# Folding query weights with a head in each half of TensorE's columns, and three moved steps, in a two-layer gated cross-attention block

## The chip, the cores and the metric

The kernel runs on one NeuronCore of one Trainium2 chip. The metric is the device time of one execution in microseconds. Three runs of the kernel before took 1539.04, 1533.52 and 1535.97 us: the median is 1535.97 us. The engines are named as in the profile: PE is TensorE (PEld its weight loads), DVE is VectorE, ACT is ScalarE, POOL is GpSimd, and SP is SyncE, which here only issues DMAs.

## The reference, cut to what matters

The model has two layers, each a gated cross-attention and a gated feed-forward part. All data are float32; x is 16 blocks of 128 tokens by 512. The change touches layer 0's attention and the first steps of layer 0's feed-forward part:

```python
# layer 0 attention: H = 16 heads, K = D_C = 128, D_CQ = 384, R = 64
q_hk  = (hidden_q @ Wq.T).reshape(b, s, H, K)
q_big = einsum('bshk,hkq->bshq', q_hk, w_kc_q)
kv_rope = kv_c * cos + rotate_half(kv_c) * sin
q_r = einsum('bshq,hqr->bhsr', q_big, W_qr)
k_r = einsum('bld,hdr->bhlr', kv_rope, W_kr)
attn = softmax(einsum('bhsr,bhlr->bhsl', q_r, k_r))
ctx_lat = einsum('bhsd,hkd->bshk', einsum('bhsl,bld->bhsd', attn, kv_rope), w_kc_kv)
out = ctx_lat.reshape(b, s, H * K) @ Wo.T

# layer 0 feed-forward: 8 experts of rank 16, two chosen per token
base_h1 = x @ W1 + b1
t1 = einsum('td,erd->ter', x, A1);  l1 = einsum('ter,efr->tef', t1, B1) * 2
a = gelu(base_h1[:, None] + l1);    mix = (a * combine).sum(1)
```

The three matrices between x and q_r (Wq, w_kc_q, W_qr) do not depend on the tokens, so they can be multiplied together once: for each head, M = w_kc_q @ W_qr is 128 x 64, and Wq_head.T @ M is 512 x 64.

## The kernel before, in words

**The query fold (lines 470 to 575).** The 16 heads are taken as 8 pairs. `load_middle(p)` (L471) loads a pair's w_kc_q, turned so that its 384 inner rows lie on partitions in three chunks (`wcq`, 384 KB a pair), and its W_qr (`wqr`, 192 KB). `load_inner(p)` (L484) loads its 256 rows of Wq (`wq`, 512 KB). All go through SP's queue, which issues in order; each tile has three buffers, so a pair's loads wait until the pair three places ahead has been used. `fold_first(p)` (L505) makes M: for each head j of the pair, three matmuls over the chunks with `wcq` of that head stationary (128 columns) and both heads' `wqr` moving (2 x 64 columns); one of the two 64-column results is the head's own, and DVE copies it to `m_sb`. `fold_second(p)` (L520) makes Wq_head.T @ M in four matmuls a head, which ACT copies to the folded weights `fq`. The first fold of pair p+1 stands ahead of the second fold of pair p (L550), so that DVE's copy has time.

In the same loop, group 0's keys and queries are made: `key` (L406, one matmul of 512 columns a pair) and `query` (L409, four a pair). Keys need the rotated latents: `load_kv(0)` (L379, called at L495, after the loads of the first pair and of the second pair's middle weights) loads them through SP, `rope` (L385) rotates them in five operations on POOL, and TensorE turns them (`kvtr`, L556). Queries need the normalised tokens: `layernorm_T` (L140) has DVE take the statistics of four blocks, normalise them (`xn`, two buffers), TensorE turn them (`xtr`), and ACT and DVE copy them out by turns (`evacuate`, L81).

**Product tiles.** PSUM is held in three pools of 512-column tiles: `mm` (four), `tr` (two) and `acc` (two). A step that takes a tile waits until the step that had it two or four places earlier has been read out.

**Layer 0's attention (lines 825 to 980)** has an order written out by hand: from L827 on TensorE, DVE's main steps and SP keep program order. `fold_outward(p)` (L592) multiplies w_kc_kv and Wo for heads p and p+8 into a near (`tr`) and a far (`acc`) tile; DVE copies part of the near product and makes two differences (L600, L605, L606), ACT copies the far product (L601), and the last difference reads both. `score(b)` makes a block's scores in four tiles; `soften(b, t)` is four exponentials on ACT with a product on POOL; `block` turns 32 x 32 blocks on DVE; `carry` moves them by DMA. `turn(v)` (L447) turns two normalised blocks through two `tr` tiles, the first copied out by ACT and the second by DVE. At L838 `turn(2)` stands ahead of `fold_next(7)`, the last outward fold.

**The step to the feed-forward part.** In the last round of the attention loop (`u == last`) the last products of the attention are made by `project(v, n)` (L718). `spread(first)` (L357, called at L952 between projects 1 and 5) makes t1 for the first group of tokens: four matmuls of 512 columns into a `tr` tile, then two scalings on DVE, one for each chosen expert, which read the tokens' choice `selT`. Behind the loop the layer's next loads are issued (x, `b2_sb`, and others), DVE makes a difference `b2_d` of the loaded `b2_sb` (L1000, the profile's `b_d`), and then `up_pair` (L1032) makes two feature chunks of base_h1 by seven products of half size each (`hs` and `ht` tiles, sums on DVE at L1053 to L1063), and `adapt_pair` (L1073) makes four `l` products from t1, adds base (L1088) and takes the gelu. `up_pair` and `adapt_pair` alternate over eight pairs of chunks.

Of the kernel before, what the change touches and what calls it, by code (L numbers as in the profile page):

```python
# [9 lines left out]
F32 = mybir.dt.float32  # L10
# [5 lines left out]
P = 128  # L16
# [7 lines left out]
NPAIR = H // 2  # L24
R = 64
QC = 3
# [16 lines left out]
def kernel(  # L43
# [9 lines left out]
    nc = tc.nc  # L53
# [9 lines left out]
    def mm_tile(name):  # L63
        return ps_mm.tile([P, 512], F32, tag="mm", name=name)

    def tr_tile(name):
        return ps_tr.tile([P, 512], F32, tag="tr", name=name)
# [13 lines left out]
    def evacuate(dst, src):  # L81

        flip[0] ^= 1
        if flip[0]:
            pin(nc.vector.tensor_copy(dst, src))  # L85
        else:
            nc.scalar.copy(dst, src)  # L87


    ident = const.tile([P, P], F32, name="ident")  # L90
# [283 lines left out]
    with tc.tile_pool(name="a0", bufs=2) as ap, tc.tile_pool(name="a0s", bufs=3) as sp:  # L374
# [4 lines left out]
        def load_kv(g):  # L379
            kv = ap.tile([P, GB, P], F32, tag="kv", name=f"kv_{g}", bufs=1)  # L380
            b = place(g * GB)
            send(kv, kvc[b : b + GB].rearrange("b l d -> l b d"))
            return kv
# [84 lines left out]
        with tc.tile_pool(name="fold", bufs=3, side="right") as fp:  # L468
            loaded = {}

            def load_middle(p):  # L471

                wcq_p = fp.tile([P, 2, QC, P], F32, tag="wcq", name=f"wcq_{p}")
                wqr_p = fp.tile([P, 2, QC, R], F32, tag="wqr", name=f"wqr_{p}")
                hs = slice(2 * p, 2 * p + 2)
                wcq_in = wcqT[hs].rearrange("h (p c) k -> p h c k", c=QC)
                wqr_in = wqr[hs].rearrange("h (p c) r -> p h c r", c=QC)

                for j in ((0, 1) if p == 0 else (slice(0, 2),)):
                    nc.sync.dma_start(out=wcq_p[:, j], in_=wcq_in[:, j])  # L480
                    nc.sync.dma_start(out=wqr_p[:, j], in_=wqr_in[:, j])
                loaded[p] = wcq_p, wqr_p

            def load_inner(p):  # L484
                wq_p = fp.tile([P, 2, D], F32, tag="wq", name=f"wq_{p}")
                nc.sync.dma_start(
                    out=wq_p,
                    in_=wq[2 * p * P : (2 * p + 2) * P, :].rearrange("(h p) d -> p h d", p=P),
                )
                loaded[p] = wq_p, *loaded[p]  # L490

            load_middle(0)
            load_inner(0)
            load_middle(1)
            kv_0 = load_kv(0)  # L495
            nc.scalar.dma_start(out=cos_sb, in_=cos_t)
            nc.scalar.dma_start(out=sin_sb, in_=sin_t)
            for n in range(GB):
                nc.scalar.dma_start(out=xs[n], in_=x[place(n)])
            nc.scalar.dma_start(out=wkr_sb, in_=wkr)  # L500
            nc.scalar.dma_start(out=gates[:, 0:2], in_=g_x.partition_broadcast(P))
            nc.scalar.dma_start(out=gates[:, 2:4], in_=g_f.partition_broadcast(P))
            nc.scalar.activation(gates, gates, AF.Tanh)

            def fold_first(p):  # L505


                _, wcq_p, wqr_p = loaded[p]
                m_sb = fp.tile([P, 2, R], F32, tag="m", name=f"m_{p}")
                for j in range(2):  # L510
                    m_ps = mm_tile(f"m_ps{p}_{j}")
                    for c in range(QC):
                        nc.tensor.matmul(
                            m_ps[:, : 2 * R], wcq_p[:, j, c, :], wqr_p[:, :, c, :],
                            start=(c == 0), stop=(c == QC - 1),
                        )
                    nc.vector.tensor_copy(m_sb[:, j, :], m_ps[:, ts(j, R)])
                return m_sb

            def fold_second(p, m_sb):  # L520
                wq_p = loaded[p][0]
                for j in range(2):
                    f_ps = mm_tile(f"f_ps{p}_{j}")
                    for c in range(ND):
                        nc.tensor.matmul(
                            f_ps[:, ts(c, P)], wq_p[:, j, ts(c, P)], m_sb,
                            start=True, stop=True,
                        )
                    nc.scalar.copy(
                        fq[:, :, ts(2 * p + j, R)],  # L530
                        f_ps.rearrange("p (c r) -> p c r", r=P)[:, :, ts(j, R)],
                    )

            load_middle(2)
            for p in range(1, 3):
                load_inner(p)
            m_next = fold_first(0)
            kvr_0 = rope(0, kv_0)
            for p in range(NPAIR):
                m_now = m_next  # L540
                if p + 3 < NPAIR:
                    load_middle(p + 3)
                    load_inner(p + 3)
                if p + 4 == NPAIR:
                    for n in range(GB, KEPT):
                        nc.sync.dma_start(out=xs[n], in_=x[place(n)])
                if p == 0:
                    fold_second(p, m_now)
                if p + 1 < NPAIR:
                    m_next = fold_first(p + 1)  # L550
                if p:
                    fold_second(p, m_now)
                else:
                    tr = tr_tile("kvtr_0")
                    for i in range(GB):
                        nc.tensor.transpose(tr[:, ts(i, P)], kvr_0[:, i, :], ident)  # L556
                    kvT_0 = ap.tile([P, GT], F32, tag="kvT", name="kvT_0", bufs=1)
                    evacuate(kvT_0, tr)
                k_ps = tr_tile(f"k_ps0_{p}")
                key(k_ps, p, kvT_0)  # L560
                for v in range(2):
                    evacuate(k_r[v][p], k_ps[:, ts(v, 2 * P)])
                if p == 0:
                    xnT_0 = layernorm_T("a0", 0)
                q_ps = tr_tile(f"q_ps0_{p}")
                query(q_ps, p, xnT_0)
                for v in range(2):
                    evacuate(q_r[v][p], q_ps[:, ts(v, 2 * P)])
                if p == NPAIR - 2:
                    deviations(2)  # L570
                    normalise(2)
                    roped_1 = rope(1, load_kv(1))
# [252 lines left out]
        def fold_next(p):  # L825
            fold_outward(p, outward[p])
            if p + 5 < NPAIR:  # L827
                outward.append(load_outward(p + 5))

        score(0)  # L830
        for p in range(7):
            fold_next(p)
            if p % 2 == 0:
                soften(0, p // 2)
                if p:
                    block(0, p // 2 - 1)
        score(1)
        turn(2)  # L838
        fold_next(7)
        block(0, 3)  # L840
        carry(0)
        soften(1, 0)
# [23 lines left out]
        last = NB // 2  # L866
        for u in range(1, last + 1):
# [80 lines left out]
            if u != last - 1:  # L948
                project(v, 1)
            soft_step(now, 3)  # L950
            if u == last:
                spread(first)  # L952
            project(v, 5)
            soft_step(now, 4)
            if u < last:
# [19 lines left out]
            if u == last - 2:  # L975
                first = measure(0)
# [481 lines left out]
    q = first  # L1458
    for g in range(NG):
        last = g == NG - 1  # L1460
        held = None
        for m in range(NF // 2):
            bases = up_pair(q, m)
            if held is not None:
                adapt(q, m - 1, held)
            held = adapt_pair(q, m, bases)
            if g > 0 and m == 3:
                for b in range((g - 1) * GB, g * GB):
                    moments1(b)
        if last:  # L1470
            deviations1(slice(0, g * GB))
            aqo_sb = wp.tile([P, 2 * ND, D], F32, tag="w16", name="aqo_sb")
            for n, w in enumerate((a_wqT, a_woT)):
                send(aqo_sb[:, n * ND : (n + 1) * ND, :], w.rearrange("(c p) d -> p c d", p=P))
            xb = fh.tile([P, H, P], F32, tag="T", name="xb_a1_0")
            standard(xb, 0, mv1, rstd1, "a1", q.mixed)
            tokens(0, xb)
        else:
            nxt = measure(g + 1)
            blocks(nxt, fh.tile([P, ND, GB, P], F32, tag="T", name=f"xb_f0_{g + 1}"),  # L1480
                   q.mixed)
            turn_blocks(nxt)
        down(q, 0)
        adapt(q, NF // 2 - 1, held)
        bias_out(q)
        second_ranks(q)
        if last:
            break
        for n in range(1, 7):
            down(q, n, {  # L1490
                2: lambda: route_parts(nxt), 6: lambda: spread(nxt),
            }.get(n))
            if n == 2:
                route(nxt)
                quarter_tokens(nxt)
            elif n == 3:
                send_chosen(nxt)
        q = nxt
# [169 lines left out]
```

## Time and profile before

| what | value |
|---|---|
| median of three runs | 1535.97 us (1533.52 to 1539.04) |
| the profiled execution's own time | 1537.8 us |
| its span, first to last instruction | 1536.0 us |
| mean granted TensorE clock | 0.996 |
| TensorE's first fold, L513 | 96 passes, 14.8 us busy |
| TensorE's second fold, L525 | 128 passes, 17.8 us busy |
| DMA moved | 161.39 MB |

The profile is of one execution; its times are counted from the start of its span. A float32 matmul shows as two passes, so 6 matmuls are x12; a transpose on TensorE shows as one. Passes overlap, and the end of each is modelled: the pace of a run of matmuls is read from the start of one group to the start of the next, not from the busy time. In the timeline a line has the start, the time to the group's end, the engine and line, what is written and read, the count, and in brackets the time that the engine stood idle before and what ended it. In the waits a line has who waited for whom, the total in microseconds, the number of waits and the longest. In the windows a line has the stretch, its length, the busy time of PE, PEld, DVE, ACT and POOL with their counts, the granted clock of TensorE, the share of the DMA engines and GB/s.

### The profile page before, as it was taken

The page shows a single profiled execution, that of the slowest core. Times are in us where ns is not written, and L with a number is a line of the kernel's source. Part 1 is how long each engine was busy: PE and PEld are TensorE (multiplying, and loading weights), DVE is VectorE, ACT ScalarE, POOL GpSimd, SP SyncE. Part 2 cuts the span into 40 slices and gives each one's busy share as a digit, 9 for nine tenths or more (in the row PEclk, how much of TensorE's full clock was granted, in tenths as well). Part 3 has the DMA queues.
Part 4 walks back from the last instruction along what each step waited for, and adds up shares of the span by engine and source line. Part 5 has one row for each costly group of instructions (what it writes and reads, how often), then busy time and mean ns, then how long its engine had stood idle before and what let it go on. Part 6 is the DMA issues. An engine that isn't in the chain of part 4 may idle for free.

```text
span 1536.0 us, 19400 instructions
## 1 busy us (share of the span) xinstructions
PE 1490.6 (97%) x6768; PEld 1005.2 (65%) x6768; DVE 837.6 (55%) x1727; ACT 433.2 (28%) x1425; POOL 435.9 (28%) x437
## 2 busy tenths in 40 slices
PE   7999999999999999999999999999999799999998
PEld 5667778878877666876687667866765344444444
DVE  2264554554565556565565557455657675666422
ACT  2262433443240222022201221122034553545210
POOL 2052533632531233114321332043222221222100
PEclk9999999999999999999999999999999999999999
DMA  8435567444546621732255114521544442233402
GB/s 280 124 86 91 143 177 176 97 113 93 99 67 159 236 72 56 164 118 72 72 141 147 69 70 118 155 73 48 157 91 110 76 67 58 31 69 56 90 14 69
DMA packets 372017, 161.39 MB, mean 105 GB/s; under 512 B 299344, under 2 KB 347216, under 8 KB 369744
## 3 DMA queue, kind: packets, MB, share of 16 engines
q1 hardware_dynamic: 370624, 158.44, 41.1%
q10 hardware_dynamic: 1296, 1.71, 0.3%
q8 instruction: 54, 0.88, 0.2%
q14 instruction: 43, 0.35, 0.1%
HBM read 106.35 MB, written 18.09 MB: 81 GB/s over the span
## 4 chain that ended last, share of the span: by engine, by line
PE 88%; DVE 5%; SPq 2%; DMA 2%; ACT 1%; issue 1%; POOL 0%; DVEq 0%; POOLq 0%; ACTq 0%
PE y_ps L165 15%; PE fy_ps L165 12%; PE q_ps L165 10%; PE t_ps L165 8%; PE l_ps L165 7%; PE hs_ps L165 7%; PE ht_ps L165 5%; PE c_ps L165 4%; PE vx_ps L165 3%; PE h_ps L165 3%; PE my_ps L165 3%; PE s_ps L165 3%; PE k_ps L165 2%; SPq L175 2%; PE o_ps L165 2%
## 5 line engine op out<-in xcount | busy, mean ns | idle before, releaser
L1092 POOL TENSOR_TENSOR near<-base,a 128x512 f32<-128x512 f32 x32 | 42.6, 1330 | 346.2 <-ACT base L1089 207.1
L197 POOL TENSOR_TENSOR e<-e,rden_a 128x512 f32<-128x512 f32 x64 | 66.5, 1039 | 245.4 <-DVE rden_a L195 242.7
L165 PE MATMUL l_ps<-t,b_sb 128*128 128x512 f32 x256 | 116.8, 599 | 3.3 <-DVE base L1053 3.3
L671 POOL TENSOR_TENSOR e<-e,rden_a 128x512 f32<-128x512 f32 x64 | 66.1, 1039 | 184.6 <-DVE rden_a L669 184.6
L165 PE MATMUL q_ps<-xnT_a,fq 128*128 128x256 f32 (+1 forms) x448 | 115.9, 410 | 0.0
L664 ACT ACTIVATE e<-s_ps,nmx_a 128x128 f32<-128x128 f32 x256 | 90.3, 385 | 81.7 <-DVE nmx_a L653 39.3
L1089 ACT ACTIVATE a<-a 128x512 f32<-128x512 f32 x64 | 40.3, 630 | 257.1 <-DVE a L1088 257.1
L190 ACT ACTIVATE e<-e,nmx_a 128x128 f32<-128x128 f32 x256 | 98.8, 387 | 32.6 <-DVE nmx_a L185 32.5
L1088 DVE TENSOR_TENSOR a<-l_ps,base 128x512 f32<-128x512 f32 x64 | 44.0, 687 | 106.4 <-PE l_ps L165 106.4
L165 PEld LDWEIGHTS q_ps<-xnT_a,fq 128*128 128x128 f32 x448 | 84.8, 190 | 24.5 <-issue 11.5
L165 PEld LDWEIGHTS l_ps<-t,b_sb 128*128 128x128 f32 x256 | 49.1, 192 | 63.7 <-issue 56.9
L1154 DVE SCALAR_TENSOR_TENSOR x<-fy_ps,gw,x 128x256 f32<-128x256 f32 x112 | 46.4, 475 | 76.4 <-PE fy_ps L165 76.4
L165 PE MATMUL fy_ps<-ring,far 128*128 128x256 f32 x384 | 87.2, 380 | 0.0
L165 PE MATMUL y_ps<-fo_raw,c 128*128 128x256 f32 x384 | 85.8, 380 | 0.9 <-DVE c L85 0.9
L738 DVE SCALAR_TENSOR_TENSOR x<-y_ps,gates,x 128x256 f32<-128x256 f32 x112 | 48.6, 476 | 64.1 <-PE y_ps L165 64.0
L165 PEld LDWEIGHTS fy_ps<-ring,far 128*128 128x128 f32 x384 | 72.6, 190 | 13.6 <-issue 3.9
L165 PEld LDWEIGHTS y_ps<-fo_raw,c 128*128 128x128 f32 x384 | 72.3, 190 | 11.1 <-ACT c L87 1.0
L165 PE MATMUL ht_ps<-T,ring 128*128 128x256 f32 x256 | 65.7, 379 | 0.0
L165 PE MATMUL t_ps<-base,a_sb 128*128 128x512 f32 x128 | 65.4, 592 | 0.0
L165 PE MATMUL t_ps<-a,a_sb 128*128 128x512 f32 x128 | 65.4, 592 | 0.0
L165 PE MATMUL q_ps<-xnT_a,aqo_sb 128*128 128x512 f32 x128 | 59.7, 617 | 4.8 <-DMA xnT_a<-late 4.8
L165 PE MATMUL y_ps<-fo_sums,c 128*128 128x256 f32 x256 | 60.8, 386 | 1.4 <-DVE c L85 0.8
(241 smaller groups left out, 2926.2 us busy)
## 6 DMA issues: line engine op xcount, KB each, us to landing
ring<-w SPq DMA_DIRECT2D x32, 896.0 KB, 4.5
eT<-eb SPq DMA_DIRECT2D x336, 64.0 KB, 2.3
ring<-w SPq DMA_DIRECT2D x16, 1024.0 KB, 5.7
ring<-in_f_w SPq DMA_DIRECT2D x12, 1024.0 KB, 5.4
late<-eb SPq DMA_DIRECT2D x80, 64.0 KB, 2.3
wq<-in_wq SPq DMA_DIRECT2D x8, 512.0 KB, 5.3
quarters<-in_f_w SPq DMA_DIRECT2D x32, 128.0 KB, 2.7
w<-sums SPq DMA_DIRECT2D x8, 512.0 KB, 3.4
```

The lines of the kernel that those rows point to most:

```text
L165: ins = nc.tensor.matmul(*args, **kw)
L175: ins = nc.sync.dma_start(out=dst, in_=src)
L190: nc.scalar.activation(dst[:, ts(i, P)], src[:, ts(i, P)], AF.Exp, bias=nmx[:, i : i + 1], accum_out=den[:, i : i + 1],)
L197: nc.gpsimd.tensor_tensor(d3, d3, rden.unsqueeze(2).to_broadcast([P, 4, P]), ALU.mult)
L664: nc.scalar.activation(e[:, ts(i, P)], s_ps[:, ts(i, P)], AF.Exp, bias=nmx[:, i : i + 1], accum_out=den[:, i : i + 1],)
L671: nc.gpsimd.tensor_tensor(e3, e3, rden.unsqueeze(2).to_broadcast([P, 4, P]), ALU.mult)
L738: pin(nc.vector.scalar_tensor_tensor(dst, y_ps, gate_x[0], dst, ALU.mult, ALU.add))
L1088: nc.vector.tensor_tensor(a, l_ps, base, ALU.add)
L1089: nc.scalar.activation(a, a, AF.Gelu_apprx_tanh)
L1092: nc.gpsimd.tensor_tensor(mix, base, second, ALU.add)
L1154: nc.vector.scalar_tensor_tensor(dst, y_ps[:, ts(i, half)], q.first[:, t : t + 1], dst, ALU.mult, ALU.add,)
```

## The change

Four edits. First, `fold_first` makes M transposed: `wqr` of a head is stationary (64 columns), `wcq` moves (128 columns), and head j writes partitions 64 j to 64 j + 63 of one 128 x 128 product, so that the two heads of a pair use the two halves of TensorE's columns; the chunks are the outer loop and the heads the inner. DVE copies the product (`m_T`), and a new step, `fold_turn`, transposes it on TensorE and copies it on DVE to the same `m_sb` as before. `fold_turn` stands at once behind the first fold for pair 0, and behind the second fold of the pair before for all others. Second, group 0's latents are loaded ahead of pair 0's Wq and pair 1's weights. Third, the last outward fold stands ahead of `turn(2)`. Fourth, the first group's `spread` stands behind the first `up_pair` instead of between projects 1 and 5.

```diff
@@ load order
             load_middle(0)
+            kv_0 = load_kv(0)
             load_inner(0)
             load_middle(1)
-            kv_0 = load_kv(0)
@@ fold_first
-                m_sb = fp.tile([P, 2, R], F32, tag="m", name=f"m_{p}")
-                for j in range(2):
-                    m_ps = mm_tile(f"m_ps{p}_{j}")
-                    for c in range(QC):
+                m_ps = mm_tile(f"m_ps{p}")[:, :P]
+                for c in range(QC):
+                    for j in range(2):
                         nc.tensor.matmul(
-                            m_ps[:, : 2 * R], wcq_p[:, j, c, :], wqr_p[:, :, c, :],
+                            m_ps[ts(j, R)], wqr_p[:, j, c, :], wcq_p[:, j, c, :],
                             start=(c == 0), stop=(c == QC - 1),
                         )
-                    nc.vector.tensor_copy(m_sb[:, j, :], m_ps[:, ts(j, R)])
+                m_T = fp.tile([P, P], F32, tag="mT", name=f"mT_{p}", bufs=1)
+                nc.vector.tensor_copy(m_T, m_ps)
+                return m_T
+
+            def fold_turn(p, m_T):
+                tr = mm_tile(f"mtr_{p}")[:, :P]
+                nc.tensor.transpose(tr, m_T, ident)
+                m_sb = fp.tile([P, 2, R], F32, tag="m", name=f"m_{p}", bufs=2)
+                nc.vector.tensor_copy(m_sb.rearrange("p j r -> p (j r)"), tr)
                 return m_sb
@@ the loop over pairs
-            m_next = fold_first(0)
+            m_next = fold_turn(0, fold_first(0))
...
                 if p + 1 < NPAIR:
-                    m_next = fold_first(p + 1)
+                    m_T = fold_first(p + 1)
                 if p:
                     fold_second(p, m_now)
...
+                if p + 1 < NPAIR:
+                    m_next = fold_turn(p + 1, m_T)
                 k_ps = tr_tile(f"k_ps0_{p}")
@@ layer 0's attention
         score(1)
+        fold_next(7)
         turn(2)
-        fold_next(7)
@@ the attention loop
             soft_step(now, 3)
-            if u == last:
-                spread(first)
             project(v, 5)
@@ layer 0's feed-forward loop
             bases = up_pair(q, m)
+            if g == 0 and m == 0:
+                spread(q)
```

Up to the scheduled part (the fold) a planner orders the instructions of each engine by the dependences; by the order that it emits, the last of pair 3's six first-fold matmuls stands behind the first query of group 0, and pair 6's middle weights are issued on SP ahead of the last of four token loads.

## The prediction

> **What bounds the kernel now.** I read the page first: its engine line and the chain of work that ended last.
>
> ```profile
> PE 1490.6 (97%) x6768; PEld 1005.2 (65%) x6768; DVE 837.6 (55%) x1727; ACT 433.2 (28%) x1425; POOL 435.9 (28%) x437
> PE 88%; DVE 5%; SPq 2%; DMA 2%; ACT 1%; issue 1%; POOL 0%; DVEq 0%; POOLq 0%; ACTq 0%
> ```
>
> TensorE is the bound: what shortens its stream, or fills one of its gaps, shortens the kernel, and what other engines gain or lose counts only through a gap. Then the waits of TensorE, for the four places that the diff touches.
>
> ```profile
> PE l_ps L165 <- DVE base L1053: 3.3, 1, 3.3
> PE kvtr L556 <- POOL kvr L400: 2.1, 1, 2.1
> PE o_ps L165 <- ACT xnT_a L87: 1.8, 1, 1.8
> PE f_ps L525 <- DVE m L517: 1.2, 1, 1.2
> ```
>
> Each of the three reorderings aims at one of the first three. Last, the granted clock, in windows: one gap pulls it to half, another does not.
>
> ```profile
> 18.00:19.00 1.00, 0.36 (x2) 0.36 (x3) 0.00 (x0) 0.00 (x0) 0.59 (x1) 0.79 1.07 371
> 21.00:22.00 1.00, 1.00 (x4) 0.59 (x3) 0.22 (x1) 0.00 (x0) 0.00 (x0) 0.50 1.05 360
> 512.00:513.00 1.00, 1.00 (x2) 0.34 (x1) 0.97 (x2) 0.99 (x2) 0.00 (x0) 0.50 1.19 386
> 97.00:99.00 2.00, 1.89 (x5) 0.88 (x6) 0.70 (x3) 1.12 (x7) 0.15 (x1) 1.00 0.00 0
> ```
>
> The column before the DMA share is the clock. It is 0.50 from 18.6 to 22.0 us, after the 2.06 us wait for kvr, and from 510.1 to 513.5 after the 3.27 us wait for base: 3.4 us each, 1.7 us lost. After the 1.82 us gap at 95 to 97 it stays at 1.00.
>
> **Part 1: the first fold in steady state.** One pair in the timeline of TensorE:
>
> ```profile
> 64.42 1.50 PE L513 MATMUL m_ps<-wqr,wcq 128*128 128x128 f32 x12
> 65.75 1.95 PE L525 MATMUL f_ps<-m,wq 128*128 128x128 f32 x16
> 67.54 1.02 PE L165 MATMUL k_ps<-kvT,wkr_sb 128*128 128x512 f32 x2
> 68.40 3.60 PE L165 MATMUL q_ps<-xnT_a,fq 128*128 128x512 f32 x8
> ```
>
> From start to start m takes 1.33 us (6 matmuls of two passes, 0.22 each), f 1.79, k 0.86, q 3.44. Afterwards the same 6 matmuls have 64 stationary columns each, two heads in the two halves. No row has 64 columns; the nearest is layer 1's values, four column groups of 32 at the same 128 rows and 128 moving columns:
>
> ```profile
> 1231.75 1.08 PE L165 MATMUL o_ps<-eT,v 128*32 128x128 f32 x32
> 1232.76 0.70 PE L165 MATMUL q_ps<-xnT_a,aqo_sb 128*128 128x512 f32 x1
> ```
>
> 16 matmuls in 1.01 us: four rounds at 0.22 are 0.88, so all four groups run at once, and 0.13 is lost on entering and leaving. For two halves: 3 rounds, 0.66 + 0.13 = 0.79 us. Bounds: 0.66 (free entry) and 1.33 + 0.13 = 1.46 (halves take turns). I take 0.79, nearest to that row: 0.54 saved. The transpose costs 0.12: eight xtr transposes go from 23.60 to 24.58. Net 0.42 us a pair.
>
> The Trainium skill, "TensorEngine Tiling (Array Packing)", section "Tiling Modes", says that a change of tiling mode drains TensorE. This case's trace agrees as far as the 0.13 us above; it gives no price, so the sum stays.
>
> DVE's two 128x64 copies (0.22 us each) become two of 128x128, between 0.22 and 0.42 (the 128x256 rows): 0.3. The one ahead of the transpose lies under f (1.79 us), the one behind it under k and q (4.3 us), and DVE is busy 1.2 to 2.0 of each 10 us from 40 to 70. If that cover were gone, a pair would pay 0.6. PSUM tiles stay at four a pair. Weight loads are still issued two pairs ahead, and DMA idles from 60 to 70. Pairs 4 to 7: 4 x 0.42 = **1.7 us**; pair 3, whose steady part before is still 5 of 6 matmuls and after only one, **0.6 us**.
>
> **Part 2: kv first, and the start.** kv's issue at 7.24 us lands 7.2 us later, at 14.4; rope takes 4 us on POOL (14.59 to 18.58), and TensorE stands.
>
> ```profile
> 18.64 1.12 PE L556 MATMUL kvtr<-ident,kvr 128*128 128x128 f32 x4 [2.06 <-POOL kvr L400]
> 19.55 1.91 PE L513 MATMUL m_ps<-wqr,wcq 128*128 128x128 f32 x8
> 27.06 3.67 PE L165 MATMUL q_ps<-xnT_a,fq 128*128 128x512 f32 x8
> ```
>
> Moved ahead of wq_0 and pair 1's loads on SP's in-order queue, kv lands about 8.9 (wq_0's 512 KB took 3.26 us, from 7.23 to 10.49; kv has half), kvr is ready by 13. Everything behind kv comes 1.6 us later until pair 1's wqr, which takes kv's old landing, 14.4: wq_0 lands at 12.1. The first fold, now short, its transpose and DVE's copy, which stands behind the fourth block's statistics (end 11.1), are done by 11.7, so the second fold waits for wq_0 and starts at 12.1 instead of 11.42. At the half speed that it shows before (0.22 us a pass until 15) it ends at 15.45. Then without gaps m_1 to 16.2, kvtr 16.7, transpose and m_2 17.65, and k at 17.7 (behind DVE's 0.69 us kvT copy) instead of 21.26. From there the chain xtr, DVE's copies and xn goes at its old pace, with 0.5 more for the transpose and m_3: q_0 at 23.05 instead of 27.06. wq_1 (landed 17.4) and pair 3's wqr (20.45) are in time. **4.0 us**, 1.7 of them the clock drop that no 2 us gap causes any more. Bound on the small side: all of the load order lost again, 1.4 (the gap less f's delay).
>
> **Part 3: fold 7 ahead of the turn, at 95 us.** Today fold 7 waits until ACT has copied the first turned block:
>
> ```profile
> 96.45 0.60 ACT L87 COPY xnT_a<-xtr_a 128x512 f32<-128x512 f32 x1
> 97.11 1.98 PE L165 MATMUL o_ps<-wo,wckv_all 128*128 128x512 f32 x4 [1.82 <-ACT xnT_a L87]
> ```
>
> The wait does not go, it changes hands. The tr tiles are two; in the new order the second xtr takes the tile of fold 7's near product, which is free only after DVE's third operation on it, and that reads what ACT copies from the far product. By the emitted order this copy stands behind all four exponentials of tile 1: they end at 97.7 (98.1 less the 0.46 that the copy among them took), the copy at 98.2, DVE's subtraction at 98.7. So TensorE runs o_ps from 94.19 to 95.9 and one xtr to 96.35, stands 2.4 us, then xtr, kvtr, and q when DVE has the last copy: 100.1 instead of 99.37. **0.75 us lost.** Bounds: 1.8 gained (all waits gone) and 0.75 + 1.7 = 2.45 lost, if this gap pulls the clock down.
>
> **Part 4: spread behind the first up_pair, at 492 to 514 us.** DVE's in-order queue holds the small subtraction b_d, which waits for a load, ahead of the base sums that free TensorE's tiles:
>
> ```profile
> 509.32 0.42 DVE L1000 TENSOR_TENSOR b_d<-b_sb 128x256 f32<-128x256 f32 x1 [4.66 <-DMA b_sb<-in_f_b2T]
> 510.59 3.42 PE L165 MATMUL l_ps<-t,b_sb 128*128 128x512 f32 x4 [3.27 <-DVE base L1053]
> ```
>
> Afterwards b_d stands behind the base sums and the first of the l sums, and its load, released by project 5, is issued 3.4 us earlier. TensorE's work is the same: y 3.46, up_pair 6.05, t 3.43, four l of 0.86. What is late next is t1: after spread both scaled copies (1.29 us for two) must end before the first l, as it takes the second of them; with 0.3 for the two hand-overs TensorE stands 1.6. From 492.49: 3.46 + 6.05 + 3.43 + 1.6 + 3.44 = 17.98, so the next hs starts at 510.5 instead of 513.85. **3.35 us**: the gap goes from 3.27 to 1.6, and a 1.6 us gap is less than the 1.82 that left the clock alone. Bound: if it drops, 1.65.
>
> **Sum.** 1.7 + 0.6 + 4.0 - 0.75 + 3.35 = 8.9 us off the profiled execution, whose own time is 1537.8 us (span 1536.0): 1528.9. That execution lies 1.8 above the median shown, 1535.97; a 2.06 us gap need not cost the clock in every run, so against the median I count less, 7.0: **1529.0 us**. Between 120 and 490 us and behind 514 nothing changes in TensorE's order, and its waits hang on its own progress.
>
> **Rivals.**
> - *The clock drops at the new 2.4 us gap (part 3).* For it: the 2.06 us gap; against: transposes stand on both sides, and 1.82 did nothing. 1529.0 + 1.7 = 1530.7. Chance 0.18.
> - *Kv first only moves the wait.* wq_0 and pair 1's weights share a DMA share of 0.96 to 1.11 between 7 and 22 us; if they hold up the second fold as long as kv did kvtr, part 2 gives 1.4 for 4.0: 1531.6. Chance 0.12.
> - *The halves take turns*, so that the change does not do what it says: 1.46 for 0.79 in seven pairs (the first hides behind wq_0), 4.7: 1533.7. Against it: the row of four groups. Chance 0.10.
> - *Slower: weight loads are exposed in every first fold.* Both halves use the same 128 rows. If a load could not run under a matmul of the other half, each of a fold's 12 passes would cost load and multiply in turn, by the o_ps rows 0.11 + 0.27 = 0.38: 4.56 us for 0.79, in seven pairs 26.4, so 1555.4. It decides from 0.066 + 7.0/84 = 0.15 us a pass. Against it: column groups of 32, also on the same rows, took 1.01/32 = 0.03 a pass. Chance 0.05. The Trainium skill, "TensorE: Matmul & The Clock Gate", Part 3, section "The mechanism", states this rule: a load overlaps with running matmuls only where row groups differ. By that rule this rival comes true; this case's trace disagrees, by the 0.03 just named.
>
> **How the numbers follow.** Forecast 0.55, rivals 0.18, 0.12, 0.10, 0.05. Range 1524.5 to 1533.5: its low end is the median less the full 8.9 and part 3's 1.8 + 0.75 gained instead of lost; above it the last rival and half of the third, some 0.2 together. A measurement here can tell about 0.3% from no change, so faster means under 1531.4: nearly all of the forecast (0.51), 0.11 of the first rival, half of the second (0.06), little of the third: 0.69. Slower (over 1540.6) 0.05, the same 0.26.
>
> **What would show it.** Right: m from start to start 0.79 us; kvtr without a wait and q_0 near 23; a wait of xtr near 96 of 2.4 us on DVE; no wait of l_ps on base and one of 1.6 us on t. Wrong: passes of m every 0.11 us one by one, f_ps waiting for wq beyond 12.1, a clock of 0.50 at 100 or 510.

## The result, and the profile after

The changed kernel took 1529.46 us, the median of ten runs (1527.97 to 1533.18); the kernel before, in ten runs on the same chip, 1535.71 (1531.18 to 1539.04). The ratio is 0.9959, with a 95% interval from 0.9949 to 0.9969: 6.3 us faster, between 4.8 and 7.8. The profiled execution took 1527.97 us, with a span of 1526.2; the one before had 1536.0. These two spans differ by 9.8 us, more than the medians; the section on the clock tells where the rest lies.

The page of the changed kernel, engine line and chain:

```profile
PE 1488.4 (98%) x6776; PEld 999.4 (65%) x6776; DVE 839.7 (55%) x1727; ACT 433.6 (28%) x1425; POOL 436.7 (29%) x437
PE 90%; DVE 4%; SPq 2%; ACT 1%; DMA 1%; issue 1%; POOL 0%; DVEq 0%; ACTq 0%; POOLq 0%
```

TensorE's busy time fell by only 2.2 us. The rest of the gain is waits: DVE's share of the chain went from 5% to 4%. The waits of TensorE say which:

```profile
PE xtr_a L170 <- ACT xnT_a L87: 2.0, 1, 2.0
...
PE l_ps L165 <- DVE t L368: 1.4, 1, 1.4
...
PE f_ps L532 <- DMA wq<-in_wq: 1.3, 1, 1.3
```

The wait of kvtr on kvr is gone, and l waits 1.4 us for t instead of 3.3 for base. The wait on xnT_a is still there, 2.0 for 1.8, and has only changed hands. The granted clock in windows:

```profile
18.00:19.00 1.00, 1.00 (x5) 0.47 (x5) 0.12 (x1) 0.12 (x1) 0.00 (x0) 1.00 1.08 362
21.00:22.00 1.00, 1.00 (x11) 0.92 (x10) 0.60 (x2) 0.83 (x2) 0.00 (x0) 1.00 1.09 362
...
94.36:97.77 3.41, 3.26 (x11) 2.33 (x9) 2.08 (x5) 2.25 (x10) 2.34 (x3) 0.50 0.17 24
512.00:513.00 1.00, 1.00 (x7) 0.87 (x6) 0.89 (x3) 0.00 (x0) 0.92 (x2) 1.00 1.11 406
```

The clock stays at 1.00 at 18 and 510, where it was 0.50 before. It is 0.50 at the new gap behind fold 7.

**A steady pair** in TensorE's timeline of the changed kernel:

```profile
52.49 0.88 PE L512 MATMUL m_ps<-wcq,wqr 128*64 128x128 f32 x12
53.30 2.05 PE L532 MATMUL f_ps<-m,wq 128*128 128x128 f32 x16
55.18 0.27 PE L522 MATMUL mtr<-ident,mT 128*128 128x128 f32 x1
55.29 1.02 PE L165 MATMUL k_ps<-kvT,wkr_sb 128*128 128x512 f32 x2
56.15 3.60 PE L165 MATMUL q_ps<-xnT_a,fq 128*128 128x512 f32 x8
59.68 0.88 PE L512 MATMUL m_ps<-wcq,wqr 128*64 128x128 f32 x12
```

From start to start m takes 0.81 us (0.79 predicted) and the transpose 0.11 (0.12). But f takes 1.88 instead of 1.79, and q, ahead of m, 3.53 instead of 3.44. A pair goes from 7.42 to 7.19 us: 0.23 saved, not 0.42.

**The start** and the two other places, in the timelines of TensorE, ACT and DVE:

```profile
11.29 3.75 PE L532 MATMUL f_ps<-m,wq 128*128 128x128 f32 x16 [1.27 <-DMA wq<-in_wq]
...
16.19 0.66 PE L563 MATMUL kvtr<-ident,kvr 128*128 128x128 f32 x4
...
23.44 3.70 PE L165 MATMUL q_ps<-xnT_a,fq 128*128 128x512 f32 x8
...
92.43 0.62 ACT L610 COPY fo_raw<-o_ps 128x512 f32<-128x512 f32 x1
92.90 0.64 ACT L87 COPY xnT_a<-xtr_a 128x512 f32<-128x512 f32 x1
93.09 0.42 DVE L615 TENSOR_TENSOR fo_sums<-fo_raw,o_ps 128x256 f32<-128x256 f32 x1 [0.95 <-ACT fo_raw L610]
93.60 0.66 PE L170 MATMUL xtr_a<-ident,xn_a 128*128 128x128 f32 x4 [2.04 <-ACT xnT_a L87]
...
503.87 3.70 PE L165 MATMUL l_ps<-t,b_sb 128*128 128x512 f32 x8 [1.38 <-DVE t L368]
```

What the second turned block waits for is ACT's copy of the first one, which ends at 93.54: in the emitted program the two blocks have the same tile. DVE's last operation on fold 7's near product, which the prediction named, ended at 93.51, almost at the same time.

To compare kernels I use starts of TensorE's instructions: q_0 (the first query), s_0 (the first score, behind all pairs of the fold), q behind the turn, and kv1tr (layer 1's first transpose of its latents). Before: 27.06, 78.01, 99.37, 1118.92. After: 23.44, 72.95, 95.03, 1112.62. So 3.6 us were gained up to q_0, 1.4 more in the pairs, 0.7 was lost at the turn, and 2.0 was gained from there to kv1tr (3.4 at the l products, less the clock drop behind the turn). From kv1tr to the end the code is the same in both, and yet 3.5 us less are spent.

### The profile page after: what moved, and what is told of

It reads as the page before. It is cut to its first block, busy times and chain, and to the rows that moved or that the text cites. A ratio compares the mean times of both kernels' runs of the same rounds, so it can differ in the third digit from the quotient of the medians.

```text
span 1526.2 us, 19417 instructions
## 1 busy us (share of the span) xinstructions
PE 1488.4 (98%) x6776; PEld 999.4 (65%) x6776; DVE 839.7 (55%) x1727; ACT 433.6 (28%) x1425; POOL 436.7 (29%) x437
## 4 chain that ended last, share of the span: by engine, by line
PE 90%; DVE 4%; SPq 2%; ACT 1%; DMA 1%; issue 1%; POOL 0%; DVEq 0%; ACTq 0%; POOLq 0%
PE y_ps L165 15%; PE fy_ps L165 14%; PE q_ps L165 10%; PE t_ps L165 8%; PE l_ps L165 7%; PE hs_ps L165 7%; PE ht_ps L165 5%; PE c_ps L165 4%; PE vx_ps L165 3%; PE h_ps L165 3%; PE my_ps L165 3%; PE s_ps L165 3%; PE k_ps L165 2%; SPq L175 2%; PE o_ps L165 1%; PE f_ps L532 1%
## 5 line engine op out<-in xcount | busy, mean ns | idle before, releaser
L190 ACT ACTIVATE e<-e,nmx_a 128x128 f32<-128x128 f32 x256 | 98.8, 387 | 33.1 <-DVE nmx_a L185 33.0
L165 PE MATMUL vx_ps<-xf,mw_sb 128*128 128x512 f32 x128 | 57.5, 599 | 3.5 <-DVE late L1404 3.5
```

The lines of the kernel that those rows point to most:

```text
L165: ins = nc.tensor.matmul(*args, **kw)
L190: nc.scalar.activation(dst[:, ts(i, P)], src[:, ts(i, P)], AF.Exp, bias=nmx[:, i : i + 1], accum_out=den[:, i : i + 1],)
```

## The experiments

The theory: each part does what the prediction says, with part 1 smaller by the price of going into the column halves and out of them, and part 3 dearer by a drop of the clock. The rivals: a part's gain is only moved to the next wait; the halves take turns; the difference is the scatter of the clock. Ratios are to the kernel before on the same chip, whose median was 1535.97 us beside the four single parts, 1536.57 beside `no_swap`, `split_turn`, `kv_second` and `halves_in_turn`, and 1535.62 beside the other four. Gains over the kernel before are worked out from the ratio and its interval; differences between two changed versions are differences of their medians.

### Each part alone

`fold_only` has the new `fold_first` and `fold_turn` in the kernel before, and nothing else. The other three:

```diff
@@ kv_only
             load_middle(0)
+            kv_0 = load_kv(0)
             load_inner(0)
             load_middle(1)
-            kv_0 = load_kv(0)
@@ spread_only
-            if u == last:
-                spread(first)
...
             bases = up_pair(q, m)
+            if g == 0 and m == 0:
+                spread(q)
@@ swap_only
         score(1)
+        fold_next(7)
         turn(2)
-        fold_next(7)
```

> The kernel before with part 1 alone: column halves and one transpose a pair. Mine, after the trace of the changed kernel: a steady pair goes from 7.42 to 7.19 us (0.23 saved, not the 0.42 predicted), and what the first pairs save is waited for again at kvtr, since kvr is ready no earlier (18.6 us); six pairs are left, 1.4 us faster than before; the gap at kvtr grows from 2.1 to some 3 us. If the price on record (0.42 a pair) holds without a wait in its way, 2.3 faster. If halves took turns, over 4 us slower. Between 1533.4 and 1534.4 by the first two for a kernel before at 1535.7.

Measured: 1536.33 us, ratio 0.9999 (0.9989 to 1.0009). Nothing is seen in the time. In the profile a pair takes 7.19 us, as expected. kvtr still waits 2.07 us for kvr (I expected some 3) and starts at 18.91; s_0 starts at 75.65, 1.0 us ahead of the 76.68 of `swap_only`, which has the old start and, in its profile, no clock drop there. A gain of 1.0 us lies inside the interval, and so does the expected 1.4: it reaches to 1.7.

> The kernel before with part 2 alone: kv loaded first. Mine: the wait of kvtr (2.06 us) goes, and with it the half clock behind it (1.7 us lost); the second fold of pair 0 starts 0.5 to 0.7 us later, as wq_0 comes later: 2.5 to 3.3 us faster if the clock always dropped at that wait, 1.4 if it seldom did. Rival, that kv first only moves the wait: within 0.7 us of before, with a wait of f_ps on wq of 2 us or more.

Measured: 1533.70 us, ratio 0.9982 (0.9972 to 0.9991): 2.8 us faster, from 1.4 to 4.3. That covers both of my prices, with a drop of the clock in every execution and in few. Its profiled execution, though, shows the rival: wq_0 landed at 13.05 us (11.15 in the changed kernel, with the same order of loads on SP), f_ps waited 3.04 us, and q_0 came at 26.00. In the other seven profiles with this order wq_0 landed at 10.96 to 11.57: it was this late in one of nine, and why is not known.

> The kernel before with part 4 alone: spread behind the first up_pair. Mine: the wait of l_ps on base (3.27 us) becomes one on t of 1.4, and the half clock from 510 to 513 goes: 3.3 us faster. Rival, that the clock dropped there only in the profiled execution: 1.6 to 1.9 us faster. Rival, that the time is given back at a later load: no difference.

Measured: 1533.90 us, ratio 0.9981 (0.9971 to 0.9990): 2.9 us faster, from 1.5 to 4.5, which covers the expected 3.3 and the first rival's 1.6 to 1.9. l waits for t, and the clock stays full at 510. Against the first rival speak the profiles: the clock fell there in all five that have `spread` at its old place (table of the clock, below).

> The kernel before with part 3 alone: fold 7 ahead of turn(2). Mine: q behind the turn starts 0.7 us later; without a drop of the clock 0.7 us slower, with one at the 2 us gap in each run 2.2 us slower. Rival, that the later start is made up at the next wait: no difference.

Measured: 1538.12 us, ratio 1.0014 (1.0006 to 1.0023): 2.2 us slower (0.9 to 3.5), the case with a drop. From s_0 to q it takes 22.08 us against 21.36 in the kernel before, 0.7 more, and the clock falls behind the gap.

### Parts 1 and 2 together

`fold_kv` is the changed kernel without parts 3 and 4.

> The kernel before with parts 1 and 2 together. Alone, part 1 gave nothing (ratio 0.9999) and part 2 0.0018. Mine: part 1's first pairs are worth something only when kvr is there in time, so together they give 3.5 to 4.5 us, more than the sum of 2.9. Rival, that the parts add up: 2.9 us.

Measured: 1532.24 us, ratio 0.9977 (0.9965 to 0.9989): 3.5 us, from 1.7 to 5.4. That does not tell the two expectations apart (2.9 and 3.5 to 4.5), and the profiles do not settle it. s_0 stands at 73.58, against 75.65 with part 1 alone, 76.94 with part 2 alone and 78.01 before; but the profile before had a clock drop at kvtr, and that of part 2 alone the late wq_0. Against the 76.68 of `swap_only`, an old start without a drop, the two parts together give 3.1 us.

### Part 3 undone, and cut in two

```diff
@@ no_swap
         score(1)
-        fold_next(7)
         turn(2)
+        fold_next(7)
@@ split_turn
         score(1)
+        turn(2, 0)
         fold_next(7)
-        turn(2)
+        turn(2, 1)
```

In `split_turn` the second argument of `turn` is the block that it turns.

> The changed kernel with part 3 undone (turn(2) ahead of fold 7 again). Mine: 0.7 us faster than the changed kernel if its 2.0 us gap costs no clock, 2.2 faster if it always does: 1527.3 to 1528.8 beside 1529.5. Rival, that the start of q there does not matter: 1529.5.

Measured: 1527.23 us, ratio 0.9947 (0.9933 to 0.9961); 2.2 us under the changed kernel's median (1.8 by the two ratios), with intervals that overlap. From s_0 to q it takes 21.37 us for 22.08.

> The changed kernel with turn(2) cut in two: the first block is turned, then fold 7, then the second block. Fold 7 then covers the copy by ACT that it waited for in the kernel before, and the second block takes its tile when DVE's last difference of fold 7 is done. Mine: a gap of some 0.7 us for 1.8 (before) and 2.0 (changed), 0.9 faster than the kernel with part 3 undone and 1.6 faster than the changed kernel, without the clock: 1527.9 or, with it, 1526.5. Rival, that the second block's tile is as late as now: the gap stays at 2 us and the time at 1529.5.

Measured: 1530.79 us, ratio 0.9965 (0.9952 to 0.9978). My theory fell here: the wait did not shrink to 0.7. From s_0 to q it takes 21.70 us, 0.3 more than with the turn first. Fold 7 has its cover, but two waits are left:

```profile
92.49 0.66 PE L170 MATMUL xtr_a<-ident,xn_a 128*128 128x128 f32 x4 [0.55 <-ACT xnT_a L87]
...
95.08 5.41 PE L165 MATMUL q_ps<-xnT_a,fq 128*128 128x256 f32 x16 [1.50 <-DVE xnT_a L85]
```

The second block waits 0.55 us for ACT's copy of the first, not for DVE's last difference of fold 7 as I had said, and q waits 1.50 for DVE's copy of the second block. In this profile the clock fell behind these gaps too.

`kv_second` is `split_turn` with `load_kv(0)` between `load_inner(0)` and `load_middle(1)`.

> As the kernel with the split turn, and kv is loaded behind wq of pair 0 but ahead of pair 1's middle weights. Mine: wq_0 lands near 10.5 instead of 11.15, so the second fold starts 0.7 us earlier, and kv near 11.2 instead of 9.8, which rope still hides (kvtr is needed at 16): 0.5 to 0.7 us faster than the split turn alone. Rival, that rope's end then comes behind kvtr's turn (kvr 1.4 us later): no gain or up to 0.7 slower.

Measured: 1530.26 us, ratio 0.9964 (0.9950 to 0.9978): 0.5 us under the median of `split_turn`, with intervals so wide that neither a gain nor none is shown. In the profile wq_0 landed at 10.06 (11.31 in `split_turn`), but f_ps started at 11.67 (11.45): in both it waited for DVE's copy of m, and in the changed kernel, where it started at 11.29, for wq_0. The second fold waits for two things that come at nearly the same time, and taking away one leaves the other.

### The halves

```diff
-                for c in range(QC):
-                    for j in range(2):
+                for j in range(2):
+                    for c in range(QC):
```

> The changed kernel with the heads as the outer loop of the first fold and the chunks as the inner: the same 12 passes, but neighbours use the same half of the columns. Mine, that two halves run at once only when neighbouring passes are on different halves: m goes from 0.81 to some 1.4 us, 0.5 to 0.6 a pair, 3 to 4 us slower than the changed kernel. Rival, that the gain comes from 64 stationary columns alone: m stays at 0.8 and the time at 1529.5.

Measured: 1532.29 us, ratio 0.9976 (0.9965 to 0.9987), 2.8 us more than the changed kernel's median, with intervals that overlap a little. The timeline of `halves_in_turn`:

```profile
62.33 1.15 PE L512 MATMUL m_ps<-wcq,wqr 128*64 128x128 f32 x12
63.41 2.05 PE L532 MATMUL f_ps<-m,wq 128*128 128x128 f32 x16
```

m takes 1.08 us for 0.81, and a pair 7.46 for 7.19. So the gain does come from two halves at work at once, and 64 columns alone do not give it. But the second half still starts before the first has ended: twelve passes one by one, at the 0.11 us of f's in the kernel before (16 in 1.79), would take 1.3. The starts of the single passes of this pair show how. They form two trains of six, in each of which the passes come 0.11 us apart once it runs, and the second train starts 0.28 us behind the first. The emitted order has all six passes of one head first, so I read the trains as the two halves; three passes of the second start ahead of the last of the first. In the changed kernel the passes start two and two, 0.007 us apart, and the next two 0.11 us later. The 1.4 that I expected was too much.

`m_twice` cuts the steady first fold in two visits: chunk 0 ahead of the second fold, chunks 1 and 2 between its two heads, behind the first head's copy. The third argument is the chunks.

```diff
-                    m_T = fold_first(p + 1)
+                    m_part = fold_first(p + 1, None, range(1) if p else range(QC))
...
+                    if j == 0 and m_part is not None:
+                        m_T = fold_first(p + 1, m_part, range(1, QC))
```

> The changed kernel with the steady first fold cut in two visits: its first chunk ahead of the second fold, the other two between the two heads of the second fold. The passes are the same. Mine: going into the two halves and out of them costs some 0.1 us each way, so a second visit adds 0.2 us a pair from pair 4 on, 0.8 to 1.0 in all: the stride of a pair 7.4 instead of 7.19 us, the time about 1530.4. Rival, that entry and exit are free and the missing 0.2 us a pair lies in the transpose alone: stride 7.19, time unchanged.

Measured: 1531.38 us, ratio 0.9966 (0.9953 to 0.9978), 1.3 us over the changed kernel beside it (`changed_again`, below), with intervals that overlap: what the second visit costs is read from the timeline. That of `m_twice`:

```profile
61.64 0.44 PE L513 MATMUL m_ps<-wcq,wqr 128*64 128x128 f32 x4
62.01 1.16 PE L536 MATMUL f_ps<-m,wq 128*128 128x128 f32 x8
63.09 0.66 PE L513 MATMUL m_ps<-wcq,wqr 128*64 128x128 f32 x8
63.68 1.16 PE L536 MATMUL f_ps<-m,wq 128*128 128x128 f32 x8
```

The same passes now take 0.37 + 0.59 = 0.96 us instead of 0.81, and f's first head, ahead of the second visit, 1.08 instead of some 0.9. A pair's stride is 7.54 us for 7.19. One visit more costs 0.35 us: the price of entry and exit is real, and above what I had thought.

### A version that beats both

`turn_apart` is the changed kernel with the turn's first block ahead of score(1) and its second behind it:

```diff
+        turn(2, 0)
         score(1)
+        turn(2, 1)
         fold_next(7)
-        turn(2)
```

> The changed kernel with the turn's first block ahead of score(1) and its second behind it, then fold 7. Each tile is then read out under other work of TensorE: no wait of fold 7 or of the second block, and q waits for DVE's copy of the second block alone. Mine: q starts some 1 us earlier after the score than in the kernel with part 3 undone, and no window with 1.6 us of work or less, so no drop of the clock: 1526.2 beside 1527.2 and 1529.5. Rival, that the copy on ACT or DVE is queued behind the exponentials or the maxima and the wait only moves to q: 1527.2 to 1528.5.

Measured: 1526.61 us, ratio 0.9935 (0.9919 to 0.9951): 10 us under the kernel before, and 3.5 under the changed kernel beside it (`changed_again`). The intervals of these two ratios overlap, but the runs themselves do not: five of 1525.92 to 1527.28 here, six of 1528.60 to 1532.51 there. The timeline of `turn_apart`:

```profile
86.89 0.60 PE L170 MATMUL xtr_a<-ident,xn_a 128*128 128x128 f32 x4
87.42 2.06 PE L165 MATMUL s_ps<-k,q 64*128 64x128 f32 x32
89.41 0.66 PE L170 MATMUL xtr_a<-ident,xn_a 128*128 128x128 f32 x4
89.90 1.88 PE L165 MATMUL o_ps<-wo,wckv_all 128*128 128x512 f32 x4
```

No line has a bracket: both copies lie under other work of TensorE, q does not wait for DVE either, and from s_0 to q it takes 19.27 us (22.08 in the changed kernel, 21.36 before): 2.1 less than with part 3 undone, where I expected 1. The wait that part 3 only passed on is gone.

### The changed kernel once more

> The changed kernel itself, beside the others on one chip. Mine: 1529.5, and the clock at the gap behind fold 7 at half in this profile too unless the edge of a 3.41 us window falls inside the gap; layer 1, which the change does not touch, 410 to 413 us from kv1tr to the end instead of the 409.1 of the first profile.

Measured: 1530.09 us, ratio 0.9958 (0.9942 to 0.9975). The clock fell behind fold 7 again, from 95.4 to 98.8. From kv1tr to the end (the start of TensorE's last matmul) it took 408.8 us, not the 410 to 413 that I expected. So the 409.1 of the first profile was no accident: the next section tells what it goes with.

### The clock, over all profiles

In each profile the half clock begins and ends on one grid of 3.413 us. In the kernel before it begins at 18.58, 510.10 and 1206.42: the distances, 491.52 and 696.32, are 144 and 204 times 3.4133. The grid lies differently in each execution. The windows of the kernel before, cut at its grid:

```profile
15.17:18.59 3.42, 1.41 (x13) 1.00 1.05 383
18.59:22.00 3.41, 3.36 (x13) 0.50 1.06 369
93.68:97.09 3.41, 1.60 (x20) 1.00 0.00 0
97.09:100.51 3.42, 3.40 (x14) 1.00 0.01 2
```

TensorE's busy time is the number behind the comma. 1.41 us in one window, and the next is granted half; 1.60, and it is not. The same three places in the other profiles, each cut at its own grid:

| place and order | busy us in the emptiest window, clock of the next |
|---|---|
| kvtr's wait, old load order | before 1.41 half; spread_only 1.53 half; fold_only 1.89 full; swap_only 1.93 full |
| turn(2) first | before 1.60 full; fold_only and kv_only 1.59 full; spread_only 1.59 half; fold_kv 1.97 full; no_swap 2.45 full |
| fold 7 first | swap_only and changed_again 1.22 half; changed kernel 1.38 half; m_twice 1.55 full; halves_in_turn 2.19 full |
| split turn | split_turn 1.37 half; kv_second 1.89 full |
| l, old place of spread | swap_only 0.26, fold_only 0.49, before 0.62, fold_kv 0.82, kv_only 1.09: all half |
| l, new place of spread | nine profiles from 2.03 to 2.56: all full |

Up to 1.41 us of work the next window was always at half, from 1.89 always full, and between 1.53 and 1.60 two of six fell. A gap of 2 us falls wholly into one window or is cut by the grid: that, and not its length alone, decides whether it costs some 1.7 us more.

The same holds for all windows of the 14 profiles, from the first record of the clock (15 to 19 us) on. Of the windows at full clock, 39 held up to 1.41 us of work, and each time the next was at half; 12 held 1.42 to 1.59, and four of them were followed by half; of the 6115 from 1.61 up none was. Behind a window at half the bar is higher: eight that were busy for 0.98 to 2.74 us were followed by a second one at half, those of 2.93 and more by the full clock. This is a reading of 14 profiles; no run set the grid.

The same grid bears on layer 1. In three profiles the clock fell at 94 to 95 us and again at 1190 to 1191 (changed kernel, changed_again, split_turn), and there, from kv1tr to the end, 408.8 to 409.6 us were needed: the half clock lay over the k products, ahead of a wait for a DMA that was there anyway. The other eleven needed 410.5 to 413.2. In the kernel before the half clock came behind that wait, over the q products. First the line of the kernel before, then that of the changed kernel:

```profile
1208.85 5.87 PE L165 MATMUL q_ps<-xnT_a,aqo_sb 128*128 128x512 f32 x8 [4.83 <-DMA xnT_a<-late]
...
1201.20 3.70 PE L165 MATMUL q_ps<-xnT_a,aqo_sb 128*128 128x512 f32 x8 [1.41 <-DMA xnT_a<-late]
```

From kv1tr this wait ended after 89.93 us before and after 88.58 in the changed kernel, and to the next product q then took 5.71 and 3.54. So of the 9.8 us between the two profiled spans 3.5 lie in code that the change does not touch: 2.2 are q at half clock, which is where the grid lay, and 1.3 a DMA wait that ended earlier. Whether the change has a part in that earlier end is not shown.

## Why the prediction was right, and which terms were off

The forecast of 1529.0 us, the sign and the range held. The sum of 7.0 against the median met 6.3; point by point:

- **Part 1, the halves: right in kind.** Both halves work at once, in 0.81 us for the predicted 0.79. This is read from the timelines and from `halves_in_turn`; in the time, part 1 alone showed nothing. Each of a fold's 12 passes takes 0.07 us, where the profile has 0.14 for a weight load of these passes: loads run under matmuls. The Trainium skill, "TensorE: Matmul & The Clock Gate", Part 3, section "The mechanism", lets a load overlap with running matmuls only where row groups differ. This trace disagrees, as both halves use the same 128 rows.
- **Part 1, the price: mis-sized.** The step "3 rounds, 0.66 + 0.13 = 0.79 us", with entry and exit in the 0.13, left out what falls on the neighbours: 0.09 us on the q ahead of m and 0.09 on the f behind it. q takes 3.53 us ahead of m, but 3.44 ahead of f (28.61 to 32.05 in the same profile). The second pass of f starts 0.21 us behind its first, and all others 0.11 apart, up to the transpose; so it is the way out of the halves, and not the transpose, that costs f its 0.09. With 0.15 inside m (0.81 less six times 0.11) one visit costs 0.33, and `m_twice` paid 0.35 for one visit more. 0.42 a pair became 0.23, and the pairs from q_0 to s_0 gave 1.4 us for 2.3.
- **Part 2, the start: nearly right, in part by luck.** q_0 at 23.44 for 23.05, k at 17.71 for 17.7. The wait for wq_0 came as said, though f started at 11.29 and not 12.1; in five of the eight profiles with this order and the new first fold, f waited last for DVE's copy of m instead. f and m_1 then took 4.9 us (to 16.19) for the forecast's 4.1, and the two errors cancel. The counted 4.0 held 1.7 for a clock drop that does not come in every execution: `swap_only`, with the old start, had none and q_0 at 25.74. Against it the gain is 2.3, and 1.7 with the q_0 of `changed_again` (24.01).
- **Part 3: the loss was seen, its cause was named wrong, its size lay at the bound.** The step "the second xtr takes the tile of fold 7's near product", which DVE frees, did not hold: the second block waited 2.04 us for ACT's copy of the first, which stood behind ACT's exponentials and its copy of fold 7's far product. That the two ended 0.03 us apart is luck. Without the clock the loss is 0.7 us (0.75 predicted), by s_0 to q in five profiles. The clock fell in three of these five, and alone the part cost 2.2 us, near the bound of 2.45. "The clock drops at the new 2.4 us gap" had a chance of 0.18 and came in three of five profiles; the argument against it, that transposes stand on both sides and 1.82 did nothing, was wrong: 1.82 did nothing because of the grid. In `spread_only`, with the same order and a wait of 1.83 us, the half clock came.
- **Part 4: right.** The gap is 1.4 us for the predicted 1.6, and the clock stays. From q behind the turn to kv1tr the six profiles with it in which q ran at full clock took 1016.2 to 1016.6 us, the kernel before 1019.6: 3.2 us for 3.35.
- **From the profiled execution to the median.** I took 7.0 instead of 8.9 because a 2 us gap need not cost the clock each time. Up to kv1tr, behind all that the change touches, the two profiles differ by 6.3 us and not by 8.9: part 1 gave 0.9 less than its term, part 2 0.4 less, and the clock behind the turn took 1.4. The allowance, made for another reason, happened to pay for these: that the forecast was nearer than its terms is luck.

The parts do not add up exactly: fold_kv, swap_only and spread_only together are 0.28% faster, the whole 0.41%. The intervals of the three allow that difference, and whether there is more in it stays open.

## What to carry to other kernels

A reordering that makes a wait change hands gains nothing by itself: ask which copy the waiting instruction needs, and put work of the bounding engine between the two, as `turn_apart` does. When small matmuls are packed into column parts, charge the way in and out to the neighbours as well, and make one long visit, not two. Gaps of some 2 us should be judged by the work left in any 3.4 us window around them, and two profiles of the same code be compared stage by stage before a difference of spans is credited to a change.

## What the runs showed of the hardware

- The clock reacts to a fixed grid of 3.413 us, and a window with up to 1.41 us of work was enough to halve the next. The Trainium skill, "TensorE: Matmul & The Clock Gate", Part 1, section "What's actually happening", gives a free-running window of 3413 ns, and the profiles agree; it names an idle window as what lowers the clock, and here windows that were up to 47% busy (1.59 of 3.41 us) did so.
- Passes of one column half do not wait for those of the other half that stand ahead of them in program order: with all of one half first, m took 1.08 us, between the 0.81 by turns and the 1.3 one by one, and its passes started in two trains, the second 0.28 us behind the first.
- A visit to the column halves, between full-width float32 matmuls, cost 0.33 us beside its passes: 0.09 on the group ahead, 0.15 inside, 0.09 on the group behind. A second visit cost 0.35 us (7.54 us a pair for 7.19).
